# Two-layer attention kernel, float32: the first layer's softmax sums of 19 groups formed by VectorE transposes and reductions with one folding product per set, in place of a product with ones per group

## The chip, the cores and the metric

The kernel runs on one core of one Trainium2 chip. The metric is device time in microseconds (us), from the first to the last instruction of an execution and what lies around it; the median of the runs stands for a kernel. Engines: TensorE (PE, its weight loads PEld), VectorE (DVE), ScalarE (ACT), GpSimd (POOL), and SyncE (SP), which issues most of the DMAs.

## The reference, cut to what matters

```python
# x: (8, 32, 32, 512) float32; N = 1024 tokens, 512 channels
# layer 0: 16 heads of 32
qkv = xt @ w_qkv                                    # xt: group-normed x
attn = softmax(einsum('bhid,bhjd->bhij', q * 32**-0.5, k), axis=-1)
out = einsum('bhij,bhjd->bhid', attn, v) ... @ w_proj + b_proj
x = x + out
# layer 1: 4 heads of 128, with relative position logits
scores = q @ k + pos
attn = softmax(scores, axis=-1)
x = x + (attn @ v) ... @ Wo
```

Both softmaxes are taken here without subtracting a maximum: exponentials are multiplied into the values, and the result is divided by the exponentials' sums at the end. Each sum and its reciprocal also go into a running check, and a second, plain kernel body runs if a sum is out of bounds; it isn't run with these inputs.

## The kernel before, in words

Activations lie transposed: channels on the 128 partitions, the 1024 tokens of a batch along the free dimension, in 4 chunks of 128 channels. Every projection of 512 by 512 is computed with seven half-size products instead of eight (`seven`, L497 and on): products go to three rotating PSUM banks x, y, z (tag "bank", 3 buffers), and VectorE adds named `a` (L511) and `b` (L519), a pair of additions (L673, L676), ScalarE copies (L506, L525, L670) and one GpSimd addition (L680) put the quarters together. Each such product is split into four column tiles of the array (L421, `by_columns`), which run beside each other.

First layer's attention (`attention_0`, L796): a chunk m holds four heads of 32 channels on four quarters of the partitions, and the 1024 queries are two halves h of 512. So a batch has 8 groups (m, h), in the order m = 0, 2, 1, 3 with two halves each, counted 0 to 7 here, and each group runs over 8 blocks j of 128 keys. A step of the loop (L867) does, for one block:

- `front`: scores of the four heads into a tile of four PSUM banks (L809; one such tile exists), and one exponential over all four (L824, 128x2048) into one of three slots of `e_room`;
- `back` for the block before: products with the values into the accumulator `acc` (L835, its bank has the tag "acc", 1 buffer), and for all blocks but the first the addition of the exponentials into the group's running sum on VectorE (L847, 128x2048). The running sum takes up the slot of the group's first block; the two other slots are used in turn. The slot of a finished sum is written again by the exponential two steps after the next group has begun;
- after the last block, ScalarE copies `acc` into the query tile q, whose queries are no longer needed (L850).

`finish` (L853) then divides. It takes the single "acc" bank for a second time: four products of the running sum with `ones` (L857), one per head, sum the 128 keys of each head and leave each sum on all 32 rows of that head. `normalise` (L749) copies it to SBUF on ScalarE (L755), turns 32x32 squares with a VectorE transpose (L757) so that only one column in 32 has to be inverted (`invert`: reciprocal L772, check L775), spreads the reciprocals again by a transpose (L787), and GpSimd multiplies q by them (L761). These tiles have the tag "rec" with 2 buffers.

The second layer (`attention_1`) already does its sums otherwise: VectorE transposes each running sum and reduces it over 32 (`added_up`, L766 and L767) into 16 columns of a tile `few`, and one product with `fold` (L1008), a matrix of identities, adds up the four quarters of the partitions for all eight groups of a batch at once. Then one reciprocal serves them all, and spreads (L787) and multiplications (L1024, `quotients`) are placed among the projections of the next batch.

The order of the work is written out by hand with generators. While `attention_0` of batch b runs, `side_by_side` places between its steps, by costs, the rest of the work: output projection and residual of the first layer of batch b-1 (w_p), output projection of the second layer of batch b-2 (w_o), then the second layer's projections of batch b-1 (queries, keys, values: w_q, w_k, w_v, with the position logits L891/L898), its attention (L1053, L1067), and the first layer's projections of batch b+1 (w_qkv). Closing parts of the second layer's attention (`closing`, with `fold_up`) run among the latter. A recording layer puts each engine's instructions in order; `tc.issue_after` holds an instruction behind a named one in that order, and `tc.keep_in_program_order` keeps a product at its place. `reader[0]` is the last addition `a` or `b`, `begun[0]` the last `a`.

Weights stream through tiles with the tag "w" (16 buffers of 1 KB a partition), loaded by SP (L247, L251) seven products ahead; a product of `project_rows` takes two tiles, one of `project_T` one.

Of the kernel before, what the change touches and what calls it, by code (L numbers as in the profile page):

```python
# [17 lines left out]
P = 128  # L18
# [3 lines left out]
SUM_BOUND = 1e20  # L22

BLOCKS = 8


@with_exitstack
def quick_path(
# [103 lines left out]
    for t in mvs:  # L132
        nc.gpsimd.memset(t, 0.0)

    n_checks = B * CC * NH + 2 * 4 + B - 2
    checks = consts.tile([P, n_checks], F32, tag="checks", name="checks")
    check_at = [0]

# [76 lines left out]
    class Stream:  # L215
# [17 lines left out]
        def fetch(self, n, i):  # L233
            m, rows, u, some = self.plan[n]
            if rows and u == 1 and not m.kept:
                self.tiles[n, i] = self.tiles[n - 1, i]
                return
            got = []
            src = m.factor(i)
            if m.kept:  # L240
                got = [src[:, c, :] if rows else src[:, c, u * P : (u + 1) * P] for c in range(HC)]
                if i == some[-1] and u == 1:
                    m.kept = None
            elif rows:
                for c in range(HC):
                    t = mem.tile([P, HN], F32, tag="w", name=f"w_{m.name}_{n}_{i}_{c}", bufs=16)
                    nc.sync.dma_start(t, src[:, c, :])  # L247
                    got.append(t)
            else:
                t = mem.tile([P, HC, P], F32, tag="w", name=f"w_{m.name}_{n}_{i}", bufs=16)  # L250
                nc.sync.dma_start(t, src[:, :, u * P : (u + 1) * P])  # L251
                got = [t[:, c, :] for c in range(HC)]
            self.tiles[n, i] = got
# [539 lines left out]
    e_room = mem.tile([P, 3, HB, NB], F32, tag="e0", name="e_room", bufs=1)  # L793
    turn, sum_at = [0, 1], [2]

    def attention_0(q, k, v, b, blocks=range(NT)):  # L796

        steps = [(m, h, j) for m in (0, 2, 1, 3) for h in range(NH) for j in blocks]
        state = {}

        def front(m, h, j):
            name = f"0_{b}_{m}_{h}_{j}"
# [50 lines left out]
        def finish(m, h, esum):  # L853
            name = f"0_{b}_{m}_{h}"
            su = psum.tile([P, NB], F32, tag="acc", name=f"sums_{name}", bufs=1)
            for r in range(HB):
                nc.tensor.matmul(  # L857
                    su[r * D0 : (r + 1) * D0, :],
                    ones,
                    esum[:, r, :],  # L860
                    start=True,
                    stop=True,
                )
            normalise(q[m][:, h * NB : (h + 1) * NB], su, name)

        pending = None
        for at in steps:  # L867
            if "ended" in state:
                finish(*state.pop("ended"))
            e = front(*at)  # L870
            if pending is not None:
                back(*pending)
            pending = (*at, e)
            yield 2
        back(*pending)
        yield 1
        finish(*state.pop("ended"))
# [113 lines left out]
    def attention_1(q, k, v, seeds, b, beside=0, final=False):  # L991
# [149 lines left out]
        for _ in range(3):  # L1141
            next(last, None)

        def closing():
            if together:
                fold_up(H1 * NH - 1, f"1_{b}")
            else:
                run(last)
            yield 0

        def quotients():
            for i in range(H1 * NH):
                late = half_done if i // 2 % 2 == 0 else closed
                run(quotient(i, late[0], nc.gpsimd))
                if i % 2:
                    yield 0

        ends.append(closing())
# [356 lines left out]
    def run(part):  # L1515
        for _ in part:
            pass
# [66 lines left out]
    plan += in_parts(WO, LAST_ALONE)  # L1584

    states = [{} for _ in range(B)]
    ends, left = [], []
    load_first(states[0])
    WV0.add_up([nc.gpsimd] * 2 + [nc.vector] * 2, nc.gpsimd, keep=True)
    fill_fold()  # L1590
# [14 lines left out]
    for b in range(B + 1):  # L1605
# [84 lines left out]
        else:  # L1690
            run(chain(*rest))
    after_last(B - 1, states[B - 1])


    close_wide()
# [492 lines left out]
```

## Time and profile before

| | |
|---|---|
| median of 3 runs | 3642.09 us (3640.19 to 3643.6) |
| the profiled execution | 3640.86 us, its span 3639.1 us |
| granted TensorE clock | 1.0 |
| L857, the sums products | 512 matmul records, 71.0 us busy, in 64 groups |
| L755, copies of the sums on ACT | 64 of 585 ns |
| L757 and L787, transposes on DVE | 64 of 704 and 64 of 706 ns |
| L772 and L775, reciprocal and check, 16 columns | 64 of 257 and 64 of 236 ns |
| L761, multiplications on POOL | 64 of 1672 ns mean, 1280 median |
| L766 and L767, the second layer's transpose and reduction | 64 of 712 and 64 of 685 ns |
| L847, running sums on DVE | 448 of 2456 ns |
| L824, exponentials on ACT | 512 of 1879 ns |

How to read it: a group of instructions is named by line, engine, operation and tiles. A float32 product is two records in the trace, and four column tiles run beside each other, so that one group's sums are eight records. PE's busy time is modelled and can hide short waits; the differences between starts show them. In the lists in order of time, the columns are start, duration, engine, line, operation with tiles (out<-in), shapes and count; brackets give the engine's idle time ahead of the instruction and what ended it.

### The profile page before, as it was taken

The numbers are of one execution on the slowest core, as the hardware profiler recorded it, in microseconds if no ns is written. First come the engines' busy times: TensorE is split into PE (matmuls) and PEld (weight loads), VectorE is DVE, ScalarE is ACT, GpSimd is POOL, SyncE is SP. The second block draws the span as 40 slices with busy tenths as digits, with TensorE's granted clock in tenths as the row PEclk, the third lists the DMA queues.
The fourth block names the chain that finished last, engine by engine and source line by source line (L and its number), as shares of the span: only waits on it lengthen the run. The fifth ranks groups of instructions, "written<-read, shape, count | busy, mean of one in ns | idle before, by whom it ended". The sixth has DMA issues, their size and how long they took to land.

```text
span 3639.1 us, 80878 instructions
## 1 busy us (share of the span) xinstructions
PE 3617.0 (99%) x33882; PEld 1232.4 (34%) x33882; DVE 2511.6 (69%) x2710; ACT 2000.6 (55%) x2285; POOL 1385.6 (38%) x880
## 2 busy tenths in 40 slices
PE   9999999999999999999999999999999999999998
PEld 4222243222433234332343323433234332323343
DVE  6788656796567955679556795667856668567546
ACT  3555666446664466544665446654566545656254
POOL 1343155231552316523174231742318312166255
PEclk9999999999999999999999999999999999999999
DMA  6233164242643426344363443625336133325376
GB/s 192 72 111 105 42 173 137 68 141 66 185 127 89 131 62 194 112 114 113 74 195 94 136 97 96 186 75 142 84 100 198 59 100 79 96 98 157 96 203 149
DMA packets 577316, 431.96 MB, mean 119 GB/s; under 512 B 274320, under 2 KB 467632, under 8 KB 575920
## 3 DMA queue, kind: packets, MB, share of 16 engines
q1 hardware_dynamic: 567952, 411.05, 41.1%
q0 software_dynamic: 2608, 13.70, 1.0%
q8 instruction: 269, 4.41, 0.5%
q10 hardware_dynamic: 6384, 1.97, 0.2%
q14 instruction: 103, 0.84, 0.1%
HBM read 334.30 MB, written 92.27 MB: 117 GB/s over the span
## 4 chain that ended last, share of the span: by engine, by line
PE 96%; DVE 2%; issue 1%; ACT 1%; POOL 0%; DMA 0%; SPq 0%; ACTq 0%; DVEq 0%; POOLq 0%
PE ps L809 15%; PE acc L835 14%; PE ps L1053 12%; PE acc L1067 12%; PE y_v L421 5%; PE y_q L421 4%; PE y_k L421 4%; PE x_v L421 3%; PE z_v L421 3%; PE z_q L421 3%; PE x_k L421 3%; PE x_q L421 3%; PE z_k L421 3%; PE y_wp L421 2%; PE y_wo L421 2%; PE sums L857 2%
## 5 line engine op out<-in xcount | busy, mean ns | idle before, releaser
L824 ACT ACTIVATE e_room<-ps 128x2048 f32<-128x2048 f32 x512 | 962.0, 1879 | 746.4 <-PE ps L809 724.9
L847 DVE TENSOR_TENSOR e_room<-e_room 128x2048 f32<-128x2048 f32 x448 | 1100.3, 2456 | 369.4 <-ACT e_room L824 367.6
L978 POOL TENSOR_TENSOR pos<-pos,columns 128x512 f32<-128x512 f32 x448 | 637.5, 1442 | 184.7 <-DMA pos<-pr 182.8
L809 PE MATMUL ps<-q,k 32*64 32x512 f32 x8192 | 592.5, 613 | 1.6 <-ACT e_room L824 1.6
L835 PE MATMUL acc<-e_room,v 128*32 128x512 f32 x4096 | 546.8, 604 | 0.0
L1053 PE MATMUL ps<-q,k 128*128 128x512 f32 x1024 | 526.4, 597 | 0.5 <-ACT ps L987 0.5
L1067 PE MATMUL acc<-e,v 128*128 128x512 f32 x1024 | 523.0, 593 | 0.0
L1056 ACT ACTIVATE e<-ps 128x512 f32<-128x512 f32 x512 | 305.7, 597 | 315.9 <-PE ps L1053 307.0
L1083 DVE TENSOR_TENSOR es<-es,e 128x512 f32<-128x512 f32 x384 | 278.7, 726 | 289.1 <-ACT e L1056 286.5
L761 POOL TENSOR_TENSOR q<-q,su 128x512 f32<-128x512 f32 x64 | 107.0, 1672 | 505.2 <-DVE su L787 478.2
L1067 PEld LDWEIGHTS acc<-e,v 128*128 128x128 f32 x1024 | 193.3, 190 | 247.6 <-issue 133.5
L1053 PEld LDWEIGHTS ps<-q,k 128*128 128x128 f32 x1024 | 190.8, 190 | 254.3 <-issue 229.7
L987 ACT COPY ps<-pos 128x512 f32<-128x512 f32 x448 | 264.9, 592 | 0.4
L809 PEld LDWEIGHTS ps<-q,k 32*64 32x64 f32 x8192 | 122.9, 129 | 396.9 <-issue 212.7
L835 PEld LDWEIGHTS acc<-e_room,v 128*32 128x32 f32 x4096 | 81.4, 108 | 412.1 <-issue 364.1
L680 POOL TENSOR_TENSOR k<-b_k,p_k 128x512 f32<-128x512 f32 x32 | 49.7, 1553 | 417.6 <-ACT p_k L525 406.8
L680 POOL TENSOR_TENSOR v<-b_v,p_v 128x512 f32<-128x512 f32 x32 | 51.5, 1609 | 342.9 <-ACT p_v L525 315.4
L1024 POOL TENSOR_TENSOR q<-q,su 128x512 f32<-128x512 f32 x48 | 97.5, 2052 | 191.8 <-DVE su L787 191.8
L680 POOL TENSOR_TENSOR q<-b_q,p_q 128x512 f32<-128x512 f32 x32 | 56.6, 1769 | 174.5 <-ACT p_q L525 160.0
L907 ACT COPY pos<-pp 32x512 f32<-32x512 f32 x128 | 104.6, 817 | 29.2 <-PE pp L898 28.0
L1081 DVE TENSOR_TENSOR es<-e,e 128x512 f32<-128x512 f32 x64 | 59.8, 934 | 67.1 <-ACT e L1056 67.1
L757 DVE STREAM_TRANSPOSE tu<-su 128x512 f32<-128x512 f32 x64 | 45.1, 704 | 77.5 <-ACT su L755 77.5
(241 smaller groups left out, 4551.1 us busy)
## 6 DMA issues: line engine op xcount, KB each, us to landing
pos<-pr SPq DMA_DIRECT2D x448, 256.0 KB, 3.5
w_qkv<-ws_qkv SPq DMA_DIRECT2D x168, 128.0 KB, 2.7
x1T<-d SPq DMA_DIRECT2D x32, 512.0 KB, 5.2
d<-x1T SPq DMA_DIRECT2D x32, 512.0 KB, 3.6
pc<-pos SPq DMA_DIRECT2D x32, 512.0 KB, 6.5
pr<-pos SPq DMA_DIRECT2D x32, 512.0 KB, 7.7
columns<-pc SPq DMA_DIRECT2D x64, 256.0 KB, 4.3
x2T<-d SPq DMA_DIRECT2D x32, 512.0 KB, 6.0
```

The costliest lines, as they stand in the source:

```text
L421: ins = nc.tensor.matmul(out[columns, :], weights[:, columns], moving, start=start, stop=stop, skip_group_check=open_sum,)
L680: nc.gpsimd.tensor_tensor(self.dst[1][1], s(b), s(p7), op=ALU.add)
L809: nc.tensor.matmul(ps[some, r, :], k[m][rows, j * P + 64 * i : j * P + 64 * i + 64], q[m][rows, h * NB : (h + 1) * NB], start=True, stop=True,
L824: exps[0] = nc.scalar.activation(e, ps, AF.Exp, scale=D0 ** -0.5)
L835: nc.tensor.matmul(acc[r * D0 : (r + 1) * D0, :], v[:, j, c0 : c0 + D0], e[:, r, :], start=(j == blocks[0]), stop=(j == blocks[-1]),)
L847: summed[0] = nc.vector.tensor_add(state["esum"], state["esum"], e)
L978: nc.gpsimd.tensor_tensor(self.rows[i], self.rows[i], self.columns[i // NT], op=ALU.add)
L987: self.copied = nc.scalar.copy(ps, rows)
L1053: scored[0] = nc.tensor.matmul(ps, k[h][:, keys], q[:, h, queries], start=False, stop=True, skip_group_check=True)
L1056: exps[0] = nc.scalar.activation(e, ps, AF.Exp, scale=1.0 / math.sqrt(D1))
L1067: nc.tensor.matmul(acc, v[:, j, h * D1 : (h + 1) * D1], e, start=(j == 0), stop=(j == NT - 1),)
L1083: added[0] = nc.vector.tensor_add(state["esum"], state["esum"], e)
```

## The change

For some groups of the first layer, those beside the second layer's projections, `finish` is not called. A new class `Apart` does the following instead. `take` transposes the running sum of each of the four heads (128x512) and reduces each over 32 into 16 columns of a new tile `few_0`: two heads at the step at which `finish` would have been called, two heads at the next step, these held behind `reader[0]`. `fold_up` adds the four quarters of the partitions with four products with `fold`, one column tile for each head, for all groups of a set, then inverts and checks them once. `quotient` spreads the reciprocals of one group and has GpSimd multiply q. `ones` is still used by the groups that call `finish`.

Which groups: none of batch 0; groups 2 and 3 of batch 1; groups 2, 3 and 4 of batches 2 to 6; groups 3 and 4 of batch 7: 19 of 64 in 7 sets. In batches 1 and 7 the fold and the quotients follow in the next steps of the same attention. In batches 2 to 6 the set is put aside, and folded in `closing` right after the fold of the second layer's attention that runs beside it; its quotients go, one for each pair of the second layer's, among the projections of the next batch. The weight tiles get 15 buffers instead of 16 (the new tile takes 768 bytes a partition), and the number of checks is smaller.

```diff
+APART = [(2, 3, 4)]
...
+    def apart_of(b):
+        if b == 1:
+            return [(2, 3)] + APART[1:]
+        return [] if b == 0 else [(3, 4)] if b == B - 1 else APART
...
-                    t = mem.tile([P, HN], F32, tag="w", name=f"w_{m.name}_{n}_{i}_{c}", bufs=16)
+                    t = mem.tile([P, HN], F32, tag="w", name=f"w_{m.name}_{n}_{i}_{c}", bufs=15)
...
+    few_0 = mem.tile([P, HB, 3, NB // 32], F32, tag="few0", name="few_0", bufs=1)
+
+    class Apart:
...
+        def take(self, m, h, esum, dst):
+            at = len(self.groups)
+            self.groups.append((m, h, dst))
+            for r0 in range(0, HB, 2):
+                turned = []
+                for r in (r0, r0 + 1):
+                    t = mem.tile([P, NB], F32, tag="rec", name=f"tu_0_{self.b}_{m}_{h}_{r}", bufs=2)
+                    with tc.issue_after(reader[0].ins) if r0 else nullcontext():
+                        nc.vector.transpose(t, esum[:, r, :])
+                    turned.append(t)
+                for r, t in zip((r0, r0 + 1), turned):
+                    nc.vector.tensor_reduce(
+                        few_0[:, r, at, :],
+                        t.rearrange("p (t c) -> p t c", c=32),
+                        axis=AX.X,
+                        op=ALU.add,
+                    )
+                yield
+
+        def fold_up(self):
+            name = f"0_{self.b}_{self.some[0]}"
+            su = bank(f"sums_{name}")[:, : self.width]
+            for r in range(HB):
+                ins = nc.tensor.matmul(
+                    su[r * D0 : (r + 1) * D0, :],
+                    fold[:, r, :],
+                    self.place(r).rearrange("p g t -> p (g t)"),
+                    start=True,
+                    stop=True,
+                )
+                tc.keep_in_program_order(ins)
+            spare = mem.tile([P, NB], F32, tag="rec", name=f"sp_{name}", bufs=2)
+            invert(self.place(0).rearrange("p g t -> p (g t)"), su, spare[:, : self.width])
+
+        def quotient(self, i, behind=None):
+            m, h, dst = self.groups[i]
+            su = mem.tile([P, NB], F32, tag="rec", name=f"su_0_{self.b}_{m}_{h}", bufs=2)
+            with tc.issue_after(behind.ins) if behind is not None else nullcontext():
+                spread(su, few_0[:, 0, i, :])
+            nc.gpsimd.tensor_tensor(dst, dst, su, op=ALU.mult)
...
+        def sums_apart(i, m, h, esum):
+            part = aparts[i]
+            together = i == 4 and b < B - 1
+            if together:
+                aside.append(part)
+            yield from part.take(m, h, esum, q[m][:, h * NB : (h + 1) * NB])
+            if together or i != part.some[-1]:
+                return
+            part.fold_up()
+            for i in range(len(part.some)):
+                yield
+                part.quotient(i)
...
             if "ended" in state:
-                finish(*state.pop("ended"))
+                if ended in aparts:
+                    ending.append(sums_apart(ended, *state.pop("ended")))
+                else:
+                    finish(*state.pop("ended"))
+                ended += 1
+            for part in ending:
+                next(part, None)
...
+        aside_0 = aside.pop() if aside else None
+
         def closing():
             if together:
                 fold_up(H1 * NH - 1, f"1_{b}")
+                if aside_0 is not None:
+                    aside_0.fold_up()
...
                 if i % 2:
+                    if aside_0 is not None and i // 2 < len(aside_0.some):
+                        aside_0.quotient(i // 2, begun[0])
                     yield 0
```

More of the change, by code (lines that the diff above doesn't have):

```diff
@@ L133, in quick_path @@
         nc.gpsimd.memset(t, 0.0)
+    def apart_of(b):
+        if b == 1:
+            return [(2, 3)] + APART[1:]
+        return [] if b == 0 else [(3, 4)] if b == B - 1 else APART
     n_checks = B * CC * NH + 2 * 4 + B - 2
+    n_checks -= sum(len(some) - 1 for b in range(B) for some in apart_of(b))
     checks = consts.tile([P, n_checks], F32, tag="checks", name="checks")
@@ L249, in fetch @@
             else:
-                t = mem.tile([P, HC, P], F32, tag="w", name=f"w_{m.name}_{n}_{i}", bufs=16)
+                t = mem.tile([P, HC, P], F32, tag="w", name=f"w_{m.name}_{n}_{i}", bufs=15)
                 nc.sync.dma_start(t, src[:, :, u * P : (u + 1) * P])
@@ L794, in quick_path, with __init__, place @@
     turn, sum_at = [0, 1], [2]
+    few_0 = mem.tile([P, HB, 3, NB // 32], F32, tag="few0", name="few_0", bufs=1)
+    class Apart:
+        def __init__(self, b, some):
+            self.b, self.some = b, some
+            self.groups = []
+            self.width = len(some) * (NB // 32)
+        def place(self, r):
+            return few_0[:, r, : len(self.some), :]
+        def take(self, m, h, esum, dst):
[36 more added lines that the diff above has]
+            nc.gpsimd.tensor_tensor(dst, dst, su, op=ALU.mult)
     def attention_0(q, k, v, b, blocks=range(NT)):
@@ L799, in attention_0 @@
         state = {}
+        aparts = {i: part for some in apart_of(b) for part in [Apart(b, some)] for i in some}
+        def sums_apart(i, m, h, esum):
[10 more added lines that the diff above has]
+                part.quotient(i)
         def front(m, h, j):
@@ L866, in attention_0 @@
         pending = None
+        ended, ending = 0, []
         for at in steps:
             if "ended" in state:
-                finish(*state.pop("ended"))
+                if ended in aparts:
[5 more added lines that the diff above has]
+                next(part, None)
             e = front(*at)
@@ L874, in attention_0 @@
             yield 2
+        for part in ending:
+            run(part)
         back(*pending)
@@ L1586, in quick_path @@
     states = [{} for _ in range(B)]
-    ends, left = [], []
+    ends, left, aside = [], [], []
     load_first(states[0])
@@ L1692, in quick_path @@
     after_last(B - 1, states[B - 1])
+    assert check_at[0] == n_checks, (check_at[0], n_checks)
     close_wide()
```

## The prediction

> **What bounds the kernel now.** I read the busy shares first, then the chain that ended last, then the order of time on TensorE around one of the products that the change takes out. The two lines of the page:
>
> ```profile
> PE 3617.0 (99%) x33882; PEld 1232.4 (34%) x33882; DVE 2511.6 (69%) x2710; ACT 2000.6 (55%) x2285; POOL 1385.6 (38%) x880
> ...
> PE 96%; DVE 2%; issue 1%; ACT 1%; POOL 0%; DMA 0%; SPq 0%; ACTq 0%; DVEq 0%; POOLq 0%
> ```
>
> TensorE (PE) is busy for 99% and is 96% of the chain. But a busy PE can hide short waits, so I looked at start times. This is PE around the end of group 2 of batch 2 (columns: start, duration, engine, line, operation):
>
> ```profile
> 854.14 1.90 PE L421 MATMUL x_q<-x1T,w_q 128*32 128x512 f32 x16
> 855.97 1.11 PE L809 MATMUL ps<-q,k 32*64 32x512 f32 x16
> 857.01 1.07 PE L835 MATMUL acc<-e_room,v 128*32 128x512 f32 x8
> 857.89 1.90 PE L421 MATMUL y_q<-f_xn,w_q 128*32 128x512 f32 x16
> 859.61 1.05 PE L857 MATMUL sums<-e_room,ones 128*32 128x512 f32 x8
> 860.59 1.11 PE L809 MATMUL ps<-q,k 32*64 32x512 f32 x16
> ```
>
> The reader is to take differences of starts: a projection block followed by scores takes 855.97 - 854.14 = 1.83 us, one followed by sums 859.61 - 857.89 = 1.72, and the sums hold PE for 860.59 - 859.61 = 0.98. Nothing waits: the same blocks have the same lengths, within 0.01 us, at nearly every place of the trace. So the kernel is as long as its list of PE work, and a product taken out is worth its slot if nothing new makes PE wait.
>
> The slot is shared with other engines' work. VectorE (DVE) around group 3 of batch 2:
>
> ```profile
> 902.83 0.69 DVE L519 TENSOR_TENSOR b_k<-y_k,p_k 128x512 f32<-128x512 f32 x1 [4.68 <-PE y_k L421]
> 907.14 0.69 DVE L673 TENSOR_TENSOR k<-y_k,p_k 128x512 f32<-128x512 f32 x1 [3.62 <-PE y_k L421]
> 908.61 0.71 DVE L757 STREAM_TRANSPOSE tu<-su 128x512 f32<-128x512 f32 x1 [0.78 <-ACT su L755]
> ...
> 910.99 3.06 DVE L847 TENSOR_TENSOR e_room<-e_room 128x2048 f32<-128x2048 f32 x1 [0.52 <-ACT e_room L824]
> ```
>
> Here the brackets say how long DVE had nothing to do: 4.68 and 3.62 us just ahead of the end of the group.
>
> **What the Trainium skill says.** (1) "TensorEngine Tiling (Array Packing)", Key Properties: changing the tiling mode drains TensorE. The trace agrees: 128*32 projections to 32*64 scores cost 1.83 - 1.72 = 0.11 us. This switch stays when the sums go (projection, sums and fold are all 128*32), so only 0.98 - 0.11 = 0.87 is won. (2) "VectorE: DVE Perf Modes", the perf-mode tier table: tensor_reduce has only the 1x mode. The trace agrees: 685 ns for 512 elements, as slow as the 712 ns transpose. (3) "SBUF — State Buffer", SBUF: two separate sides: a DVE instruction with two SBUF inputs and a GpSimd one lock each other out for an instruction. The trace agrees: the L847 addition takes 2.29 us mostly, 3.06 at 910.99, where POOL's multiplication L761 starts at 910.62.
>
> **The change, part by part.** 19 of the 64 groups (2 of batch 1, 3 each of batches 2 to 6, 2 of batch 7) go the new way. In the order of PE's instructions nothing else changes: 19 sums out, 7 folds in.
>
> *Sums out.* In all 19, the slot is 0.97 to 1.00 us before scores; less the 0.11 of the switch, 0.86 each: 19 x 0.86 = 16.3 us off the path. In one of them, batch 7's group 4, PE also waits:
>
> ```profile
> 3145.93 1.90 PE L421 MATMUL y_k<-f_xn,w_k 128*32 128x512 f32 x16
> 3148.62 1.06 PE L857 MATMUL sums<-e_room,ones 128*32 128x512 f32 x8 [0.79 <-ACT q L850]
> 3149.62 1.11 PE L809 MATMUL ps<-q,k 32*64 32x512 f32 x16
> ```
>
> The sums need the one "acc" bank, that is ScalarE's copy L850. Without them the scores wait only for the exponential that reads their banks (3146.21 + 1.88 = 3148.09). From 3149.62 to about 3148.15 are 1.47 us, 0.6 more than the slot. Sum so far 16.9.
>
> *Folds in.* Four products of 32 or 48 columns, eight records. The nearest row is the second layer's fold:
>
> ```profile
> 1066.20 1.92 PE L421 MATMUL x_q<-x0T,w_qkv 128*32 128x512 f32 x16
> 1068.05 0.49 PE L1008 MATMUL sums<-few,fold 128*128 128x128 f32 x2
> 1068.47 1.11 PE L809 MATMUL ps<-q,k 32*64 32x512 f32 x16
> ```
>
> It costs 1068.47 - 1066.20 - 1.83 = 0.44 us with a full 128x128 weight load. The other bound is the logits' products L891/L898: eight records of 128 columns start within 0.22 us, so 48 columns take 0.1. I take 0.15 for the two folds among projections and 0.3 for the five right behind an L1008 fold (one more switch, 0.11): 2 x 0.15 + 5 x 0.3 = 1.8 us; bounds 0.7 and 3.1.
>
> *ScalarE and GpSimd.* 19 copies L755 of 0.585 us go, all off the path; the "acc" bank of the next group comes free earlier. GpSimd's 19 multiplications stay, but 15 of them move to the next batch's query projection, beside the second layer's own.
>
> *VectorE.* Each group gets 4 transposes of 0.71 and 4 reductions of 0.69 = 5.6 us, loses one transpose (0.71), reciprocal and check (0.26 + 0.2). Net 19 x 4.4 = 84, plus 7 small reciprocals and checks (0.6 each, 4) = 88 us on an engine that is idle for 31% of 3639 = 1128 us. What hides it is idle time at the place, so I laid the eight into DVE's time by hand. The first two transposes and reductions stand right after the last addition, the other two behind one addition `a` or `b` of the projection. What is queued behind: the addition that frees a projection bank (read again 7 us later or more) and the next L847. What waits: the exponential two steps on, which writes the old sum's slot of e_room. Taking 0.86 off starts after the sums, the last transpose ends, and that exponential would start, at:
> - batches 2 to 6, group 2: 862.0 against 866.4; group 3: 904.9 against 915.6; group 4: 948.6 against 952.5;
> - batch 1: group 2 425.5 against 427.6; group 3 477.0 against 476.2, so late by 0.8;
> - batch 7: group 3 3108.4 against 3110.6; group 4 3147.9 against 3157.
>
> Only one is late; there PE has about 0.8 us until it next wants the banks (with the fold), so it may lose 0 to 0.3. If the cover were gone everywhere, all 5.6 us a group would show, 106 us.
>
> *Five folds set aside.* DVE now does two reciprocals before the check that frees the second layer's fold bank, and the next projection takes just that bank: 1068.58 + 0.96 + 0.45 + 0.3 = 1070.3, wanted at 1070.4 plus the fold. A tie: 0 to 0.4 us each. The three spreads per batch come third in a row on two buffers ("rec"), so each waits in DVE's queue for a multiplication by GpSimd: 1080.5 to 1083.0 in batch 2, and twice more. Queued behind each is an L847 addition, later by 2.6 to 3.1 us. It ends at 1086.7, and the exponential that needs its slot comes at 1088.15; the projection's addition behind the third ends at 1111.3, its bank is wanted at 1113.6. So these hold DVE, not PE. For all new waits together I take 0.5 us, bounds 0 and 7.
>
> *Weight buffers 16 to 15.* Loads on SP's queue: at most 14 ahead and one in use, so 15 suffice; some issue one product later. Landing takes 2.1 to 3.6 us, the lead is six products or more (over 10 us). Zero; if the cover is gone, 1 to 3 us a batch.
>
> *Sum.* 16.9 - 1.8 - 0.5 = 14.6 us. The profiled execution took 3640.9 (span 3639.1 and 1.8 around it): 3626.3. The median of the runs is 1.2 higher, 3642.1 - 14.6 = 3627.5.
>
> **The rivals.**
> *R1, the waits reach PE in part.* The 15 held spreads and 5 ties: if each spread costs PE 0.4 us and each tie 0.3, that is 7.5 us, and 7.1 are left: 3635. For it: two buffers for three tiles, and scores with one projection block between them leave the exponential only some 0.3 us. Against: the margins of 1.4 and 2.3 us above.
> *R2, slower: the old sum's slot.* If the second pair of transposes ends one projection block too late in each group, the exponential is late and the scores behind it wait for their banks: 19 x 1.83 = 35 us lost, 20 net: 3662. For it: the second pair stands behind an addition that itself waits for PE, and batch 1's group 3 is already late. Against: margins of 2 us or more in 18 of 19. It decides from 14.6 / 19 = 0.77 us of lost PE time per group.
> *R3, nothing is won.* If PE was waiting at these places anyway, the slot would be filled by a wait: 3642. Against: only one of the 19 has a wait in front, and the blocks behind keep their lengths.
>
> **How the numbers follow.** Forecast 0.68, R1 0.14, R3 0.08, R2 0.10. The forecast's own range is 3624 (folds and waits at their lower bounds: 16.9 - 0.7 = 16.2 gives 3625.9, less 2 us of scatter between runs) to 3632; R1 reaches from there to 3639. 3623.5 to 3637 holds some 8 in 10. A measurement of this kernel tells about 0.2% (7.3 us) from no change, so faster begins below 3634.8: the forecast and half of R1, 0.75; same: the other half, R3, 0.15; slower: R2, 0.10.
>
> **What would show it.** Right: L857 has 360 matmul records (45 x 8) instead of 512; scores follow y_q directly at 1.83 us; about 88 us more on DVE; PE's list shorter by 15 us and PE idle no longer. A fold slot of 0.1 to 0.45 us. Wrong: new PE waits on "ACT e_room L824" two steps after such a group (R2), or on DVE behind the spreads (R1), or L421 blocks longer than 1.72 with a weight load as releaser.

## The result, and the profile after

| | before | after |
|---|---|---|
| median of 5 runs | 3641.11 us (3640.19 to 3643.6) | 3625.74 us (3623.57 to 3626.75) |
| ratio, 95% interval | | 0.9956 (0.9943 to 0.9969) |
| the profiled execution, its span | 3640.86, 3639.1 us | 3626.2, 3624.4 us |
| PE busy, matmul records | 3617.0 us, 33882 | 3604.8 us, 33786 |
| products with ones (L857, now L934) | 512 records | 360 records |

The change takes 15.4 us off the median, 0.44%; the forecast was 14.6 less, at 3627.5 us. The changed kernel has other line numbers: sums are L934 (L857 before), scores L886 (L809), exponentials L901 (L824), products with the values L912 (L835), running sums L924 (L847), projections L430 (L421). New are transposes L826, reductions L829, folds L841 and multiplications L857.

The busy shares and the chain of waits, as before the change:

```profile
PE 3604.8 (99%) x33786; PEld 1230.2 (34%) x33786; DVE 2573.9 (71%) x2807; ACT 1990.6 (55%) x2266; POOL 1399.2 (39%) x880
...
PE 96%; DVE 2%; ACT 1%; issue 1%; DMA 0%; POOL 0%; SPq 0%; DVEq 0%; ACTq 0%; POOLq 0%
```

PE is 99% busy and 96% of the chain, as it was: the list of PE's work became shorter, and PE still waits for almost nothing. VectorE went from 69 to 71%.

PE in order of time at the end of group 2 of batch 2, the place shown before:

```profile
855.41 1.07 PE L912 MATMUL acc<-e_room,v 128*32 128x512 f32 x8
856.29 1.90 PE L430 MATMUL y_q<-f_xn,w_q 128*32 128x512 f32 x16
858.12 1.11 PE L886 MATMUL ps<-q,k 32*64 32x512 f32 x16
```

The projection is now followed by the scores, 858.12 - 856.29 = 1.83 us on. Before, 2.70 us lay between the same two (857.89 to 860.59): 0.87 less. I laid the PE lists of the two traces side by side, product by product, and took the difference of start times. It steps by 0.86 or 0.87 at 18 of the 19 places, by 1.42 at the 19th, batch 7's group 4, where PE had also waited for ScalarE's copy.

One of the five folds that were put aside, in the same kind of list:

```profile
1062.02 1.92 PE L430 MATMUL x_q<-x0T,w_qkv 128*32 128x512 f32 x16
1063.87 0.49 PE L1094 MATMUL sums<-few,fold 128*128 128x128 f32 x2
1064.29 0.29 PE L841 MATMUL sums<-few,fold 128*32 128x48 f32 x8
1064.51 1.11 PE L886 MATMUL ps<-q,k 32*64 32x512 f32 x16
```

Its slot is 1064.51 - 1064.29 = 0.22 us. The two folds that lie among projections moved the difference by only 0.06 each.

VectorE around group 3 of batch 2, the place shown before:

```profile
891.54 2.29 DVE L924 TENSOR_TENSOR e_room<-e_room 128x2048 f32<-128x2048 f32 x1 [0.34 <-ACT e_room L901]
893.86 1.30 DVE L826 STREAM_TRANSPOSE tu<-e_room 128x512 f32<-128x512 f32 x2
...
900.36 0.69 DVE L528 TENSOR_TENSOR b_k<-y_k,p_k 128x512 f32<-128x512 f32 x1 [3.44 <-PE y_k L430]
900.97 1.29 DVE L826 STREAM_TRANSPOSE tu<-e_room 128x512 f32<-128x512 f32 x2
902.19 1.24 DVE L829 TENSOR_REDUCE few<-tu 128x16 f32<-128x512 f32 x2
```

The first two transposes start at once behind the last addition of the running sum, the other two behind an addition `b`, and even so VectorE is idle for 3.44 us between them. The last transpose ends at 902.26; the exponential that overwrites the old sum started at 913.09.

Two things were not foreseen, and they pull in opposite directions. At the start of batch 7's second layer PE had a stretch at half its clock, which it did not have in the profiled execution of before, and which cost 3.0 us (the last section tells when it comes):

```profile
3184.00:3188.00 4.00, 2.96 (x30) 0.57 (x26) 3.74 (x3) 2.37 (x2) 4.00 (x3) 1.00 0.70 258
3188.00:3192.00 4.00, 4.00 (x8) 1.09 (x8) 1.57 (x1) 1.09 (x2) 3.92 (x2) 0.65 0.91 331
3192.00:3196.00 4.00, 4.00 (x14) 0.98 (x12) 1.22 (x1) 1.09 (x2) 2.66 (x2) 0.50 0.22 73
3196.00:3200.00 4.00, 4.00 (x19) 1.02 (x14) 1.49 (x1) 2.96 (x3) 1.54 (x2) 0.99 0.16 59
```

These are stretches of 4 us with the busy time of PE, PEld, DVE, ACT and POOL (number of records in brackets), then PE's granted clock, the DMA share and GB/s. The clock is 0.65 and 0.50 in two of them; the same stretches of before, 3200 to 3216, have 1.00 throughout. The other thing is the tail, the work behind the second layer of batch 7. Before, one of the last products waited 0.91 us for ScalarE's copy L590; after, it did not, and by the starts this is 1.0 us less. The copy stands behind six DMA issues on ScalarE's own queue, here in before and then in after:

```profile
3621.07 4.63 ACTq L1450 DMA_DIRECT2D out<-ot  x6
3608.42 3.33 ACTq L1542 DMA_DIRECT2D out<-ot  x6
```

In the 14 traces these six issues take 3.3 us in six and 4.5 to 5.3 us in eight. Among the eight are three kernels that have all of the change's new work (e5, e6 and e8 below), so the shorter issues are not simply what the change brings; why they differ stays open. From the last transposes to the end it took 8.05 us instead of 9.06. Over the 14 traces this lies between the same two values, so the 1.0 us here looks like scatter. So the span fell by 17.0 (sums) - 1.3 (folds and small shifts) + 2.0 (tail) - 3.0 (clock) = 14.7 us by these steps, which is what was measured.

### The profile page after: what moved, and what is told of

It reads as the page before. It is cut to its first block, busy times and chain, and to the rows that moved or that the text cites. A ratio compares the mean times of both kernels' runs of the same rounds, so it can differ in the third digit from the quotient of the medians.

```text
span 3624.4 us, 80755 instructions
## 1 busy us (share of the span) xinstructions
PE 3604.8 (99%) x33786; PEld 1230.2 (34%) x33786; DVE 2573.9 (71%) x2807; ACT 1990.6 (55%) x2266; POOL 1399.2 (39%) x880
## 4 chain that ended last, share of the span: by engine, by line
PE 96%; DVE 2%; ACT 1%; issue 1%; DMA 0%; POOL 0%; SPq 0%; DVEq 0%; ACTq 0%; POOLq 0%
PE ps L886 15%; PE acc L912 14%; PE ps L1139 12%; PE acc L1153 12%; PE y_v L430 5%; PE y_q L430 4%; PE y_k L430 4%; PE z_v L430 3%; PE x_v L430 3%; PE z_q L430 3%; PE x_k L430 3%; PE x_q L430 3%; PE z_k L430 3%; PE y_wp L430 2%; PE y_wo L430 2%; PE x_wp L430 2%
## 5 line engine op out<-in xcount | busy, mean ns | idle before, releaser
L901 ACT ACTIVATE e_room<-ps 128x2048 f32<-128x2048 f32 x512 | 962.0, 1879 | 749.8 <-PE ps L886 728.1
L924 DVE TENSOR_TENSOR e_room<-e_room 128x2048 f32<-128x2048 f32 x448 | 1093.4, 2441 | 375.2 <-ACT e_room L901 373.7
L886 PE MATMUL ps<-q,k 32*64 32x512 f32 x8192 | 594.0, 613 | 2.1 <-ACT e_room L901 2.0
L912 PE MATMUL acc<-e_room,v 128*32 128x512 f32 x4096 | 546.8, 604 | 0.0
L886 PEld LDWEIGHTS ps<-q,k 32*64 32x64 f32 x8192 | 123.1, 130 | 394.7 <-issue 201.2
L912 PEld LDWEIGHTS acc<-e_room,v 128*32 128x32 f32 x4096 | 81.4, 108 | 412.6 <-issue 366.2
L770 POOL TENSOR_TENSOR q<-q,su 128x512 f32<-128x512 f32 x45 | 70.3, 1563 | 352.0 <-DVE su L796 328.0
L1110 POOL TENSOR_TENSOR q<-q,su 128x512 f32<-128x512 f32 x48 | 76.8, 1621 | 180.2 <-DVE su L796 180.0
L1064 POOL TENSOR_TENSOR slots<-slots,columns 128x512 f32<-128x512 f32 x64 | 84.0, 1341 | 22.2 <-DMA slots<-pr 22.1
```

The costliest lines, as they stand in the source:

```text
L886: nc.tensor.matmul(ps[some, r, :], k[m][rows, j * P + 64 * i : j * P + 64 * i + 64], q[m][rows, h * NB : (h + 1) * NB], start=True, stop=True,
L901: exps[0] = nc.scalar.activation(e, ps, AF.Exp, scale=D0 ** -0.5)
L912: nc.tensor.matmul(acc[r * D0 : (r + 1) * D0, :], v[:, j, c0 : c0 + D0], e[:, r, :], start=(j == blocks[0]), stop=(j == blocks[-1]),)
L924: summed[0] = nc.vector.tensor_add(state["esum"], state["esum"], e)
L1064: nc.gpsimd.tensor_tensor(self.rows[i], self.rows[i], self.columns[i // NT], op=ALU.add)
```

## The experiments

The kernel before took 3640.0 to 3640.6 us (medians) beside these runs. "Lower times" are the lower of two clusters of times, of which the last section tells.

| kernel | median, us | ratio to before, 95% interval |
|---|---|---|
| e1_buffers | 3640.76 | 1.0002 (0.9993 to 1.0011) |
| e2_turn_only | 3686.94 | 1.0132 (1.0115 to 1.0149) |
| e3_no_sums | 3623.22 | 0.9953 (0.9937 to 0.9970) |
| e4_double | 3632.50 | 0.9976 (0.9967 to 0.9984) |
| e5_first_two | 3667.81 | 1.0074 (1.0058 to 1.0091) |
| e6_late_two | 3650.66 | 1.0025 (1.0015 to 1.0036) |
| e7_in_place | 3623.55 | 0.9953 (0.9939 to 0.9966) |
| e8_product_back | 3641.95 | 1.0005 (0.9997 to 1.0014) |
| e9_third_rec | 3714.09 | 1.0200 (1.0183 to 1.0217) |
| e10_six_alone | 3619.59 | 0.9943 (0.9930 to 0.9957) |
| e11_more | 3619.22 | 0.9941 (0.9928 to 0.9955) |
| e12_without_first | 3618.94 | 0.9939 (0.9926 to 0.9953) |

**The buffers alone.** The changed kernel with no group chosen:

```diff
-        if b == 1:
-            return [(2, 3)] + APART[1:]
-        return [] if b == 0 else [(3, 4)] if b == B - 1 else APART
+        return []
```

> The changed kernel with no group chosen: all 64 groups divide as before, few_0 is allocated and unused, and the weight tiles have 15 buffers. Theory (the sixteenth buffer is spare, since at most 14 are ahead and one is in use): 3641.1 us, as before, within 2. Rival (the loads lose their lead and PE waits for weights): 1 to 3 us a batch, so 3649 to 3665; the changed kernel would then hide a gain that much larger.

It took 3640.76 us, as before. The sixteenth weight buffer was spare. (13 are too few: in e9_third_rec below PE waited for weights 6 times, once for 20.6 us.)

**The product alone, put back.**

```diff
-        def finish(m, h, esum):
+        def finish(m, h, esum, apart=False):
...
+            if apart:
+                nc.scalar.copy(unread, su[:, :16])
+                return
             normalise(q[m][:, h * NB : (h + 1) * NB], su, name)
...
-                    ending.append(sums_apart(ended, *state.pop("ended")))
+                    done = state.pop("ended")
+                    finish(*done, apart=True)
+                    ending.append(sums_apart(ended, *done))
```

> The changed kernel with the 19 products with ones put back in their old place, their result only touched by a copy of 16 columns on ScalarE and used for nothing; the sums still come from VectorE and the folds, and no division is added. Theory (the gain is the slot of the product and nothing else): back by 18 x 0.86 + 1.42 = 16.9 us from the changed kernel's lower times of 3623.7, so 3640.6, with the single waits 3640 to 3644. Rival A (the gain is partly from the smaller load on ScalarE or VectorE, which stays): less than 12 us back, under 3636. Rival B (the loss of 46 us in e2_turn_only came from the product and the turning of the same sum together): over 3655.

It took 3641.95 us; 9 of its 12 runs lie at 3641.5 to 3642.8. That is the kernel before (3640.4) and the folds (1.3): my 3640.6 took the changed kernel's tail for a gain of the product and so was 1 us low. All of VectorE's new work is in it, and next to none of it shows: besides the folds and the half-clock stretch, its PE list ends up later than that of before by some 0.3 us (a wait of 0.27 us for ScalarE's copy of the position logits in batch 6 is most of it). So the gain is the slot of the product: not ScalarE's smaller load (rival A), and the product and the turning of one sum don't hinder each other (rival B).

**No division at all for the 19 groups.**

```diff
-                    ending.append(sums_apart(ended, *state.pop("ended")))
+                    state.pop("ended")
...
```

> Leaves out the division of the 19 groups altogether: no sums, no transposes, no folds, no multiplication. This gives the whole worth of the 19 slots. Theory (each slot is 0.86, batch 7's group 4 1.42 to 1.47, nothing else on the path): 16.9 us less than before, 3624.2, about 1.4 less than the changed kernel, which is the folds alone (5 x 0.22 + 2 x 0.06 + 0.04). Rival (the new work on VectorE and GpSimd costs the changed kernel some us in stalls that the slots hide): 3 us or more less than the changed kernel, 3622 or below. Another (part of the gain is from elsewhere, as the tail): over 3626.

3623.22 us, 17.3 less than the kernel before beside it, where 16.9 was worked out. Against the trace of the changed kernel its PE list is shorter by 0.22 at each of the five put-aside folds, by 0.06 at the two others, and by nothing else that belongs to the change (the half-clock stretch is missing from it, and the tail's 1.0 is back). So the changed kernel's new work costs PE the folds, 1.2 us, and no stall.

**VectorE's work twice.** Each transpose and each reduction of the 19 groups is issued two times:

```diff
                         nc.vector.transpose(t, esum[:, r, :])
+                        nc.vector.transpose(t, esum[:, r, :])
...
-                    nc.vector.tensor_reduce(
+                    for _ in range(2):
+                        nc.vector.tensor_reduce(
...
```

> The changed kernel with each transpose and each reduction of the 19 groups issued twice, so that each costs VectorE about 11 us rather than 5.5. Theory (idle time at the place covers it, with margins before the exponential of 4.4, 10.7 and 3.9 us in batches 2 to 6, 2.1 and -0.8 in batch 1, 2.2 and 9 in batch 7): the 5.5 us more eat up the margins of groups 2 and 4, which come 1 to 2 us late, less what the next VectorE additions can catch up: 12 groups by 0.5 to 1.8, so 6 to 20 us more than the changed kernel, 3632 to 3646. If VectorE's work stays wholly hidden: 3626, and the margins were underestimated. If nothing was hidden: 104 us more, 3730.

3632.5 us, within the range that I gave, but not by the way that I gave. PE's list comes later by 2.1 us behind batch 1's group 2, by 1.7 at that batch's fold, and by 2.7, 1.4 and 0.3 in batch 7: 8.2 in all, of which the 1.4 is a stretch at half clock behind the wait. Apart from the fold, which had to wait for its last reduction, these are the places with the smallest forecast margins, 2.1 and 2.2. But what PE waits for there is not the exponential to which those margins were reckoned; it is a projection's addition in VectorE's queue behind the transposes:

```profile
434.96 1.92 PE L430 MATMUL y_k<-f_xn,w_k 128*32 128x512 f32 x16 [1.96 <-DVE b_k L528]
...
3110.47 3.33 PE L430 MATMUL y_k<-f_xn,w_k 128*32 128x512 f32 x16 [2.50 <-DVE a_k L520]
```

In batches 2 to 6, 15 of the 19 groups, it is later by only 0.1 us behind each group 4. I had expected groups 2 and 4 there to come late. Their margins before the exponential fell from 4.7 and 4.5 us to 2.2 and 1.0, by less than the added work. So at 15 places twice the work is still covered. Of the exponentials only two waited for a transpose, 4.0 us in all, as their group shows (busy and mean ns, then the idle time ahead by what ended it):

```profile
L903 ACT ACTIVATE e_room<-ps 128x2048 f32<-128x2048 f32 x512 | 962.1, 1879 | 756.4 <-PE ps L888 735.3 <-DVE e_room L926 12.3 <-DVE tu L827 4.0
```

**Product, division and turning together.** A first attempt to add VectorE's work alone:

```diff
-                    ending.append(sums_apart(ended, *state.pop("ended")))
+                    done = state.pop("ended")
+                    finish(*done)
+                    ending.append(aparts[ended].take(*done, None))
...
```

> The 19 groups keep their product with ones and their division, and VectorE also turns and reduces their sums into few_0, which nothing reads. So only the work on VectorE is added, about 19 x 5.0 = 95 us by the measured reductions. Theory (VectorE has idle time at these places, and no exponential comes late): 3641 us, at most 1 more. R1 (its waits reach PE in part): 0.4 us a group, 3649. R2 (the exponential that takes the slot of the old sum comes one block late): 19 x 1.83 = 35, 3676.

3686.94 us, 46 more than before, and so a miss. It did not add the work at the same place: `finish` comes first, and the transposes are queued behind its division. VectorE at the end of group 4 of batch 2 (idle time and what ended it in brackets):

```profile
957.37 0.71 DVE L765 STREAM_TRANSPOSE tu<-su 128x512 f32<-128x512 f32 x1 [2.51 <-ACT su L763]
...
959.83 0.71 DVE L825 STREAM_TRANSPOSE tu<-e_room 128x512 f32<-128x512 f32 x1
962.86 0.71 DVE L825 STREAM_TRANSPOSE tu<-e_room 128x512 f32<-128x512 f32 x1 [2.32 <-POOL q L769]
```

and ScalarE there:

```profile
966.04 1.88 ACT L900 ACTIVATE e_room<-ps 128x2048 f32<-128x2048 f32 x1 [6.33 <-DVE tu L825]
```

VectorE stands idle for 2.51 us until the sums are copied, divides, and stands again for 2.32 us, since GpSimd still holds a "rec" buffer; the exponential that overwrites the old sum comes 6.33 us late. That is rival R2 of the prediction with its mechanism: in this trace 13 exponentials wait for transposes, 54.0 us in all.

I took the two "rec" buffers for the cause and gave the tag a third at all its places, with 13 weight buffers to make room:

```diff
-        su = mem.tile([P, NB], F32, tag="rec", name=f"su_{name}", bufs=2)
+        su = mem.tile([P, NB], F32, tag="rec", name=f"su_{name}", bufs=3)
...
-                    t = mem.tile([P, HN], F32, tag="w", name=f"w_{m.name}_{n}_{i}_{c}", bufs=15)
+                    t = mem.tile([P, HN], F32, tag="w", name=f"w_{m.name}_{n}_{i}_{c}", bufs=13)
```

> e2_turn_only (product, division and turning all together, 3686.9) with three buffers of the tag rec instead of two, and 13 weight buffers to make room. There a transpose waited for GpSimd, which held a rec buffer with its multiplication behind three multiplications of the position logits, and the exponential of the old sum's slot came 6 us late in five batches. Theory (the pair of buffers was the cause, not VectorE's work): 3641 to 3650; what stays is the lateness of batch 1 and batch 7, at most 8 us. Rival (VectorE's queue itself is too long at the end of group 4): 3675 or more.

3714.09 us: my theory that the pair of buffers was the cause falls. (What I called GpSimd's multiplications of the position logits are additions, L1065.) The rise itself comes mostly from the weights, for which PE waited 24.4 us, with a stretch of 20.48 us at half clock around the longest of these waits. But at the place in question the exponential still waited 5.19 us where it had waited 6.33:

```profile
981.92 0.71 DVE L765 STREAM_TRANSPOSE tu<-su 128x512 f32<-128x512 f32 x1 [2.51 <-ACT su L763]
...
988.66 0.71 DVE L825 STREAM_TRANSPOSE tu<-e_room 128x512 f32<-128x512 f32 x1 [1.32 <-POOL q L769]
989.30 1.24 DVE L828 TENSOR_REDUCE few<-tu 128x16 f32<-128x512 f32 x2
989.47 1.88 ACT L900 ACTIVATE e_room<-ps 128x2048 f32<-128x2048 f32 x1 [5.19 <-DVE tu L825]
```

The third buffer took 1.1 us off here, and the waits of exponentials for transposes fell from 54.0 to 31.7 us in the whole trace. It did not end the buffer's part, since the last transpose still waits 1.32 us for GpSimd. What it left as it was is the 2.51 us for ScalarE's copy, with the division behind it. In the changed kernel the product, its copy and the division are gone from ahead of the transposes, so that they start right behind the last addition; and in e8_product_back, where the product stands there but not the division and its copy of the whole sum, no exponential of batches 2 to 6 waits for a transpose. So what the change takes away is part of what makes its new work fit.

**Other groups.** The first two groups of batches 2 to 6 also, where VectorE is busiest:

```diff
-        return [] if b == 0 else [(3, 4)] if b == B - 1 else APART
+        return [] if b == 0 else [(3, 4)] if b == B - 1 else [(0, 1)] + APART
```

> The changed kernel with groups 0 and 1 of batches 2 to 6 also taken by VectorE, as a set folded in the next steps. There VectorE is busy for 105 to 107% of the time (by the profile, records overlapping) in the 16 us after a group's end, against 58 to 79% at groups 2 to 4. If VectorE's time cost nothing anywhere: 10 x 0.86 - 5 x 0.06 = 8.3 us less, 3615.4. Theory (no cover here): each of the ten brings VectorE 4.4 us behind, PE waits for its additions or for the exponential by 2 to 5 us each: 3635 to 3670, slower than the changed kernel.

3667.81 us, 42 more than the changed kernel. Each of the ten products gave its 0.86 back and more was lost behind it: PE waited for additions of the residual (L469, L705) and L520 of VectorE, 31 us in all by the trace, and in three of the five batches a stretch at half clock followed.

Groups 5 and 6 of batches 2 to 6, in place of 0 and 1, besides those of the change:

```diff
-        return [] if b == 0 else [(3, 4)] if b == B - 1 else APART
+        return [] if b == 0 else [(3, 4)] if b == B - 1 else APART + [(5, 6)]
```

> The changed kernel with groups 5 and 6 of batches 2 to 6 also taken by VectorE, as a set folded in the next steps. VectorE is busy for 79 and 74% of the 16 us after their ends, as at group 4. Theory (cover as at groups 2 to 4): 10 x 0.86 - 5 x 0.06 = 8.3 us less than 3623.7, 3615.4, with the single waits up to 3619. Rival (the transposes share two rec buffers with the spread quotients of the second layer, which wait for GpSimd just there, so that VectorE is held as in e2_turn_only): five times 2 to 6 us lost, 3625 to 3645.

3650.66 us: the rival, and above its range. Here are VectorE, ScalarE and PE behind group 5 of batch 2:

```profile
1098.00 1.30 DVE L796 STREAM_TRANSPOSE su<-few 128x512 f32<-128x512 f32 x2
1100.94 0.71 DVE L796 STREAM_TRANSPOSE su<-few 128x512 f32<-128x512 f32 x1 [1.64 <-POOL q L1110]
1102.16 0.71 DVE L826 STREAM_TRANSPOSE tu<-e_room 128x512 f32<-128x512 f32 x1 [0.51 <-POOL q L1110]
1103.38 0.71 DVE L826 STREAM_TRANSPOSE tu<-e_room 128x512 f32<-128x512 f32 x1 [0.51 <-POOL q L857]
```

```profile
1104.18 1.88 ACT L901 ACTIVATE e_room<-ps 128x2048 f32<-128x2048 f32 x1 [5.88 <-DVE tu L826]
```

```profile
1106.12 2.01 PE L886 MATMUL ps<-q,k 32*64 32x512 f32 x16 [4.76 <-ACT e_room L901]
```

Three spread quotients stand ahead of the second pair of transposes. The third of them and then both transposes find no free buffer and wait for GpSimd (1.64, 0.51, 0.51 us). The last transpose ends at 1104.09, the exponential starts at 1104.18 after 5.88 us of waiting, and PE loses 4.76 us. Its first products after that take 2.01 us instead of 1.11: half clock again. So R1's spreads and R2's old slot are one chain, and it is real, at this place. Group 6 of the same kernel gained its 0.86 in all five batches with nothing lost but the fold's 0.06. That led to the next one, with group 6 without group 5:

```diff
-        return [] if b == 0 else [(3, 4)] if b == B - 1 else APART
+        return [] if b == 0 else [(3, 4)] if b == B - 1 else APART + [(6,)]
```

> The changed kernel with only group 6 of batches 2 to 6 taken by VectorE as well, each as a set of its own folded in the next step. In e6_late_two group 6 gained its 0.86 each time with no wait behind it, and all the loss came at group 5, where the spread quotients of the second layer stand in VectorE's queue. Theory (the place decides, not the amount of VectorE's work): 5 x (0.86 - 0.06) = 4.0 us less than the changed kernel at the same granted clock, 3619.7 at its lower times, 3622 with the half-clock stretch. Rival (VectorE is near its limit, each further group costs more than it gives): 3626 or more.

3619.59 us, four of five runs at 3619.5 to 3619.9, against 3619.7 expected. It beats both kernels. So here the place decides, not the amount of VectorE's work: PE's list is shorter by 0.86 five times less 0.06 for each fold, and its waits for exponentials are as they were:

```profile
PE ps L886 <- ACT e_room L901: 1.9, 4, 1.0
```

(us in all, number, the longest; 2.0, 4 and 1.0 in the changed kernel.) Two variants with more groups:

```diff
-            return [(2, 3)] + APART[1:]
-        return [] if b == 0 else [(3, 4)] if b == B - 1 else APART
+            return [(2, 3), (6,)]
+        return [] if b == 0 else [(3, 4), (5, 6)] if b == B - 1 else APART + [(6,)]
```

> As e10_six_alone, and group 6 of batch 1 and groups 5 and 6 of batch 7, which end beside the next batch's projections and beside the second layer's attention. Theory (group 6 of batch 1 is like those of batches 2 to 6: 0.8; in batch 7 VectorE is busy for 70% of the 16 us after these ends: 2 x 0.86 - 0.06): 2.5 us less than e10_six_alone, 3617.2 at the lower times. Rival (in batch 7 PE follows the second layer's exponentials step by step, so a late addition or exponential shows at once): 1 to 6 us more than e10_six_alone.

3619.22 us, lower times 3618.6. Batch 1's group 6 won 0.86 and lost 1.22, batch 7's groups won 0.86 and 0.97 and lost 0.58 and 0.20: between the two expectations. e12_without_first is the same with batch 1 as in the changed kernel:

```diff
-        return [] if b == 0 else [(3, 4)] if b == B - 1 else APART
+        return [] if b == 0 else [(3, 4), (5, 6)] if b == B - 1 else APART + [(6,)]
```

> As e11_more, but with group 6 of batch 1 divided by the product again. In e11_more that group won 0.86 and then lost 1.22, since a transpose and a statistics instruction of the next batch's input stood in VectorE's queue ahead of its second pair, so that the exponential of the old slot came late; groups 5 and 6 of batch 7 won 0.86 and 0.97 and lost 0.58 and 0.20. Theory (a group is worth its slot less the lateness of that one exponential, and groups don't influence one another): 0.4 us less than e11_more, 1.0 less than e10_six_alone, 3618.2 to 3618.6 at the lower times. Rival (the steps seen in single traces are chance): as e10_six_alone, 3619.5, or above.

3618.94 us, 3618.21 to 3619.19, so 0.3 above the range that I expected, with two of the five runs inside it. Its trace shows PE's list 0.99 us shorter than that of e10_six_alone, as expected; the times (3618.9 against 3619.6, runs that scatter by 1) point the same way, but don't prove it alone. Against the kernel before it is 21 us.

**The folds' place.**

```diff
-            together = i == 4 and b < B - 1
+            together = False
```

> The changed kernel with the sets of batches 2 to 6 folded in the next steps of their own attention instead of behind the second layer's fold, and their quotients one to a step. Theory (a fold among projections costs 0.06, one behind the second layer's 0.22; the quotients have idle time): 5 x 0.16 = 0.8 us less than the changed kernel, 3622.9 at the lower times. Rival (the quotients and the fold's check come in the few steps in which VectorE is behind): 5 x 1 to 3 us more, 3629 to 3639.

3623.55 us, all runs within 3623.4 to 3624.0. It does not answer what it was made for: the folds came out at the same place in PE's list, right behind the second layer's fold, because the attention of the second layer has the steps between. Only the quotients moved, and that moved no start on PE behind them by more than 0.12 us (but for the half-clock stretch, which it lacks). So where the quotients stand costs PE nothing there; why a fold among projections is cheaper (0.06 against 0.22) was not tested apart. Two other traces point to the product ahead of it: in e11_more and e12_without_first the fold of batch 7's groups 5 and 6 stands behind a product 128*128 of the second layer, with no other fold ahead, and adds 0.20.

## Why the prediction was right, point by point

*What bounds the kernel.* Right. PE's list set the end before and after, and a product was worth the difference of starts. e8_product_back, which puts the products back, lands within 0.3 us of the kernel before and the folds, so little room is left for another cause.

*Sums out, 16.9.* Right: 18 steps of 0.86 or 0.87 and one of 1.42 (1.47 forecast) are 17.0. The tiling-mode switch that stays is in these 0.86: a projection followed by scores still takes 1.83.

*Folds in, 1.8.* Somewhat too dear: five of 0.22 (0.3 assumed) and two of 0.06 (0.15) are 1.2.

*VectorE hidden.* Right in its effect. The margins, worked out by hand as the time from the last transpose to the exponential that overwrites the old sum, can be read from the trace after:

| group | forecast | measured |
|---|---|---|
| batches 2 to 6, group 2 | 4.4 | 4.7 |
| group 3 | 10.7 | 10.8 |
| group 4 | 3.9 | 4.5 |
| batch 1, group 2 | 2.1 | 2.4 |
| batch 1, group 3 | 0.8 late | 0.6 late |
| batch 7, group 3 | 2.2 | 2.9 |
| batch 7, group 4 | 9.1 | 9.5 |

The one that I called late is the one exponential of the table that waited for a transpose. It started at 476.01, where the start of before, 477.06, less the 1.66 that PE's list had won by then, gives 475.40 (ScalarE stood idle for 1.06 us ahead of it, of which 0.44 is there before too). The only step of PE's list behind it is the 0.06 of the fold, so nothing is left of the "0 to 0.3 us". The size of VectorE's work was over-stated: transposes took 687 and reductions 658 ns, 5.4 us a group rather than 5.6, and busy time rose by 62 us, not 88. Records of one group overlap a little, so that its eight instructions fill only 4.9 us of busy time (19 x 0.7 = 13 us of the gap); the additions of the running sum became 15 ns shorter on the mean (448 of them, 6.7 us); the remaining 6 us I did not take apart. Two things I did not see. The margins hold only because the transposes are the first thing behind the last addition (e2_turn_only, e6_late_two). And where they run out, it need not be the exponential that shows first: in e4_double PE waited for additions of a projection.

*Waits behind the spreads and at the five folds, 0.5.* No step of PE shows any. The spreads were held by GpSimd, 15 times and 15.7 us in all, 1.0 each where I had 2.5 in batch 2, and VectorE had the time. R1 is out at these places, and real at group 5.

*Weight buffers, 0.* Right (e1_buffers).

*R2.* Did not happen. Its price was set too low: a late exponential costs not one projection block of 1.83 us but what the queue in front of the transposes makes it, 4.8 us in e6_late_two, and with the half clock that follows 6.6 us a time (33 us lost in five batches, by the steps of PE's list and its 8.6 gained).

*The sum.* 14.6 forecast against 15.4 by the medians. At an equal clock the change is worth 15.7 by PE's steps, and 1 to 2 more come from the tail, where ScalarE's six DMA issues took 1.3 us less and the end 1.0 less, neither forecast nor explained; the half-clock stretch, which is in the profiled execution and, by their times, in two more of the five, takes up to 3.0 back. So the agreement within 0.8 us is in part two accidents that cancel. The forecast of the time itself, 3627.5, was 1.8 too high: it also stood on a median of three runs that lay 1.0 above that of five.

## What to carry to other kernels

On an engine that is busy for 99% of the time, price a removed product by the difference of starts around it, and pay attention to what stays (here the switch of tiling mode). For work moved to another engine, don't go by that engine's busy share: take the place, note the last writer before and the first overwriter after, and count everything that is queued in between, above all instructions that themselves wait for a third engine; VectorE's share in the 16 us behind groups 5 and 6 is 70 to 80% for both in the trace of after, and one lost 6.6 us a time where the other lost nothing. Compare traces start by start, and check the granted clock before giving a few us a cause.

## What the runs showed of the hardware that was not expected

*Half-clock stretches.* The traces record PE's granted clock in stretches. Besides the end of the kernel, at half clock in all of them, those at half clock are 3.41 us long, or a multiple (6.83, 20.48). The Trainium skill, "TensorE: Matmul & The Clock Gate", Part 1, says that the clock is gated by a free-running window of 3413 ns, and halved after an idle window. The lengths agree. So do the places: within each of the 14 traces all changes of the clock lie on one grid of 3.413 us, to 0.01 us, from the start to the end of the kernel.

But it does not take an idle window; here the runs differ from the page, and they decide. I took PE's busy share in every window of the grid in all 14 traces, by the records, without the first 20 us and the last 10. Of the 14,756 windows at full clock, PE was busy for 0.42 or less in 22, and the clock is halved at the end of every one of them. Of the others (0.425 and more) four have a halving at their end. So a wait shorter than a window can be enough, and whether it is depends on how it lies on the grid: the wait of 2.39 us in e5_first_two comes in five batches alike, and the clock fell in the three in which the emptiest window was busy for 0.30 to 0.32, not in the two with 0.50 and 0.53. In e6_late_two a stretch cost 1.5 to 2.1 us a time besides its wait of 4.8 to 5.0.

The four exceptions are all at one place, the stretch in batch 7. It follows a wait of 1.04 us, in a window with a share of 0.70:

```profile
3187.18 1.07 PE L886 MATMUL ps<-q,k 32*64 32x512 f32 x2 [1.04 <-ACT e_room L901]
```

All 14 traces have this wait; after, e5_first_two, e8_product_back and e11_more have the stretch. In these four the wait begins 0.16 to 0.32 us into a window of the grid, in the ten others 0.33 to 3.10 us into one. So the phase of the window decides here, and it is not the program's: the grid begins at another place against the start of the kernel in every trace (by 0.01 to 3.39 us). Why a share of 0.70 is enough at this place is open. PE's work behind the wait is thin (2 records of scores in 1.07 us, where a full block has 16 in 1.11), but that this counts was not tried.

*Two clusters of times.* The 53 distinct times of the kernel before in all comparisons lie 37 between 3639.7 and 3641.5, and 12 between 3642.9 and 3644.0, about 3 us apart, with 4 between. 3.0 us is what the half-clock stretch cost in the trace of after, and the profiled executions of after, e8_product_back and e11_more, which have it (3626.2, 3644.7, 3622.05), lie in the upper part of their runs. The mean granted clock, on record for 49 of these runs, points to the same cause: it is 1.0 in 22 of 35 of the lower cluster and in none of 11 of the upper. It is not shown, since no execution of before from the upper cluster was profiled. For a change of 0.4% this is a fifth of the effect, and it depends on chance which cluster a median of five falls in.
